# Block 0's input loaded and normalized by slots, and three edits of the early order

## The chip, the cores and the metric

The kernel runs on one core of one Trainium2 chip. Its time is the device time in microseconds (us) of one execution; the median of several runs is compared. The core has a matrix engine (TensorE, PE in the profile), a vector engine (VectorE, DVE), an activation engine (ScalarE, ACT), a general engine (GpSimd, POOL), a queue that issues most transfers (SyncE, SP), and 16 DMA engines that move the data. Each engine works through its own list of instructions in order, and waits for others by semaphores.

## The reference

A conditioned block of a transformer, for x of 2 x 2048 x 512 and a condition t of 2 x 512, all in f32:

```python
emb = silu(t) @ ada_w + ada_b                       # 512 -> 6 * 512
shift_msa, scale_msa, gate_msa, shift_mlp, scale_mlp, gate_mlp = split(emb, 6)
norm  = ln(x) * (1 + scale_msa) + shift_msa
h     = gelu(norm @ ssm_w1 + ssm_b1)                # 512 -> 512
x     = x + gate_msa * (h @ ssm_w2 + ssm_b2)        # 512 -> 512
norm2 = ln(x) * (1 + scale_mlp) + shift_mlp
hf    = gelu(norm2 @ ff_w1 + ff_b1)                 # 512 -> 1024
x     = x + gate_mlp * (hf @ ff_w2 + ff_b2)         # 1024 -> 512
```

`ln` subtracts the mean of the 512 features and divides by the root of the variance plus a small constant (1e-6; the kernel's EPS is 1e-5).

## The kernel before

The 4096 tokens are cut into eight blocks of 512. In a block each of the 128 partitions holds four tokens, one in each of four slots (`C = 4`), so that a slot is a 128 x 512 tile. A block passes four stages: `hA_i` (the first product of the SSM part, with gelu), `oA_i` (its second product, added to x), `hC_i` (the first product of the feed-forward part) and `oC_i` (the second). The products are done in f32 by schemes with fewer multiplications: a stage of type A has seven products P1 to P7 of half size, whose operands are sums of quarters; these sums are made by VectorE and GpSimd beside TensorE. `hC` has 26 products with sums called a (of the weights) and b (of the tokens).

Ahead of each type of product stands a LayerNorm (class `Norm`; `n1_i` ahead of hA_i, `n2_i` ahead of hC_i). Its steps are statistics (on VectorE by `bn_stats` and `bn_aggr`, or on ScalarE by a sum and a sum of squares with an accumulator), a root (`ve`, variance plus EPS, then a power of -0.5 on GpSimd), some small operations that sharpen the root by a Newton step and give `rstd` and `nmr`, the normalization of each slot, a transposition, and the modulation by scale and shift. For block 0's first norm the transposition is done by TensorE (`transpose`, L911) into four PSUM tiles `pts`; for the others by VectorE's turns (`turn`, L887) and transfers from `blocks` into `nT` (`move`, L895).

The modulation rows emb come from ada_w by small products on TensorE (`pada`). For the first two sixths they are made early: `rows_01` multiplies rows of 128 of ada_w (k = 0 to 3; `ada_01`), and `modulation_01` turns the result and adds the bias. The bias rows, cond and the other small vectors come in one tile `rows` by four small transfers on ScalarE's queue and are transposed on TensorE into `rowsT`, from which ScalarE copies them to `colsT`.

Until the first data are there TensorE multiplies the identity matrix by itself (`warm`, L1651).

The order of everything is written by hand. Loads stand on SP's queue in the order x_0 (two halves), ada's rows 0 and 1, 2, half of row 3, half of w1, the other half of row 3, the other half of w1, x_1, ada_2, four small gate biases, w2, b2, ada_3, ada_4, fw1. The transfers use eight semaphores in turn. From hA_0 on, `PLAN` names for each stage and each place behind a product (P1, P2, ...) which side operations are emitted there; `BY` names their engines. Names that matter here: `n1_1.stats`, `n1_1.root`, `n1_1.rest` (block 1's first norm), `gate_2.0` (modulation rows of the SSM gate and the addition of their bias on VectorE, L455) and `gate_2.1` (their spreading on TensorE, `pgate`, L462), `n1_1.sum` (operand sums of block 1), `n2_0.stats` (statistics of block 0's second norm), `n2_0.root`, `mods.0` and `mods.1` (the turned modulation rows 3 and 4 with their biases, L443 and L447), `rows.2` (modulation rows 5 on TensorE).

Lines that the trace names: L305 load of x, L348 and L355 of ada's first rows, L323 of w1, L336 to L339 the four small transfers, L418 `rows_01`, L431 and L435 `modulation_01`, L748 and L749 statistics on VectorE, L777 and L788 on ScalarE (sum, sum of squares), L812 and L813 the root, L836 to L840 block 0's small operations, L853 to L861 the others', L876 and L880 normalization, L932 and L934 modulation on ScalarE and VectorE, L500 operand sums, L709 the products of type A, L997 to L1021 what follows them, L1052 the addition to x.

Of the kernel before, what the change touches and what calls it, by code (L numbers as in the profile page):

```python
# [36 lines left out]
F32 = mybir.dt.float32  # L37
AF = mybir.ActivationFunctionType
ALU = mybir.AluOpType
EPS = 1e-06  # L40
# [103 lines left out]
        "P6": "n1_1.stats.5 n1_1.root.0 gate_2.0 n1_1.rest.0 n1_1.normal.0",  # L144
# [98 lines left out]
def kernel(  # L243
# [57 lines left out]
    def load_x(i, pieces=1):  # L301
        xs[i] = big_tile(f"x_{i}")
        for s in range(pieces):
            c = slice(s * C // pieces, (s + 1) * C // pieces)
            nc.sync.dma_start(out=xs[i][:, c, :], in_=x_blk[i][:, c, :])  # L305
# [38 lines left out]
    load_x(0, 2)  # L344
    ada_01 = [big_tile(f"ada_{h}").rearrange("p (k g) n -> p k (g n)", g=2) for h in range(2)]

    def load_ada_01(ks):
        nc.sync.dma_start(  # L348
            out=ada_01[ks[0] // 2][:, ks[0] % 2 : ks[-1] % 2 + 1],
            in_=ada_w[ks[0] * P : (ks[-1] + 1) * P, : 2 * D].rearrange("(k p) n -> p k n", p=P),  # L350
        )
# [8 lines left out]
    load_ada_01((0, 1))  # L360
    load_ada_01((2,))
# [373 lines left out]
    class Norm:  # L735
# [94 lines left out]
        def first_steps(self):  # L830

            n, v = self.name, nc.vector
            self.rstd, self.nmr = [small.tile([P, C], F32, tag=t, name=f"{t}{n}") for t in ("rstd", "nmr")]
            room = ps_t.tile([P, D], F32, tag="t", name=f"small{n}")
            a, b = room[:, :C], room[:, C : 2 * C]
            v.tensor_scalar(a, self.mv[:, :, 1], EPS, None, ALU.add)  # L836
            v.tensor_tensor(b, self.r, a, ALU.mult)
            v.scalar_tensor_tensor(b, b, -0.5, self.r, ALU.mult, ALU.mult)
            v.scalar_tensor_tensor(self.rstd, b, 1.5, self.r, ALU.add, ALU.mult)
            v.scalar_tensor_tensor(self.nmr, self.mv[:, :, 0], -1.0, self.rstd, ALU.mult, ALU.mult)  # L840
# [786 lines left out]
    def run(ops):  # L1627
        for op in ops:
            op()
# [19 lines left out]
    def warm(count, blocks=2):  # L1649
        for _ in range(count):  # L1650
            nc.tensor.matmul(  # L1651
                idle[:, :blocks],
                ident,
                ident.unsqueeze(1).to_broadcast([P, blocks, P]),
                start=True,
                stop=True,
            )

    warm(IDLE - 1, C)
    nc.tensor.transpose(pt[:, :ROWS], rows, ident[:ROWS, :ROWS])  # L1660
    warm(1, C)
    warm(1, 1)

    run(n1[0].stats())
    n1[0].root()
    nc.scalar.copy(colsT, pt[:, :ROWS])

# [3 lines left out]
        colsT[:, R_COND:R_ADA].rearrange("p (b k) -> p b k", b=B),  # L1671
        AF.Silu,
    )

    n1[0].first_steps()
# [3 lines left out]
    rows_01(pada_01, (0, 1))  # L1679
    for c in range(C):  # L1680
        n1[0].normal(c, nc.vector if c % 2 else None, on_pe=True)
    for g in (1, 4):
        rows_g = colsT[:, R_ADA + g * KD : R_ADA + (g + 1) * KD]
        nc.vector.tensor_scalar(rows_g, rows_g, 1.0, None, ALU.add)
# [113 lines left out]
    later("n2_0.stats", 9, lambda: sum(n2[0].split_stats(), []))  # L1798
# [411 lines left out]
```

## Time and profile before

| | us |
|---|---|
| median of 3 runs | 575.63 (575.44 to 576.18) |
| the profiled execution, in all | 576.39 |
| its span, first to last instruction | 574.3 |
| TensorE busy | 568.2 |
| first product of hA_0 | 14.10 |
| first product of hA_1 | 43.65 |

A row of the timeline gives the start in us, the duration, the engine, the line, the operation, out<-in, how many instructions are merged, and in brackets the idle time before and what released it. A row of the chain gives start, duration and what. The profile's engine "PE" is TensorE, "SPq" and "ACTq" are the instructions that issue transfers. A row of a table by windows gives the window, its length, the busy time of PE, PEld, DVE, ACT and POOL with the number of instructions, the granted clock of TensorE, the share of the DMA engines' time and GB/s. A row of waits gives who waited for whom: us in total, times, the longest.

### The profile page before, as it was taken

The numbers are of one execution on the slowest core, as the hardware profiler recorded it, in microseconds if no ns is written. First come the engines' busy times: TensorE is split into PE (matmuls) and PEld (weight loads), VectorE is DVE, ScalarE is ACT, GpSimd is POOL, SyncE is SP. The second block draws the span as 40 slices with busy tenths as digits, with TensorE's granted clock in tenths as the row PEclk, the third lists the DMA queues.
The fourth block names the chain that finished last, engine by engine and source line by source line (L and its number), as shares of the span: only waits on it lengthen the run. The fifth ranks groups of instructions, "written<-read, shape, count | busy, mean of one in ns | idle before, by whom it ended". The sixth has DMA issues, their size and how long they took to land.

```text
span 574.3 us, 10316 instructions
## 1 busy us (share of the span) xinstructions
PE 568.2 (99%) x3495; PEld 512.4 (89%) x3495; DVE 443.5 (77%) x992; ACT 306.2 (53%) x612; POOL 452.8 (79%) x477
## 2 busy tenths in 40 slices
PE   8999999999999999999999999999999999999997
PEld 4888888898899889998899988998889999899897
DVE  4898899657789376986869877996768588897676
ACT  2628559566834875448724688335655431732430
POOL 1699897996897869897899989998993888379261
PEclk9999999999999999999999999999999999999999
DMA  8968330414305503383032921242240240031002
GB/s 318 392 199 285 93 87 6 98 54 179 68 9 155 212 2 74 102 260 117 1 92 63 349 86 24 51 126 114 92 110 1 111 136 14 0 74 75 0 1 74
DMA packets 26992, 61.79 MB, mean 108 GB/s; under 512 B 5136, under 2 KB 6716, under 8 KB 25276
## 3 DMA queue, kind: packets, MB, share of 16 engines
q1 hardware_dynamic: 23040, 55.67, 30.0%
q10 hardware_dynamic: 3900, 5.47, 3.8%
q8 instruction: 28, 0.46, 0.3%
q14 instruction: 24, 0.20, 0.1%
HBM read 35.42 MB, written 9.97 MB: 79 GB/s over the span
## 4 chain that ended last, share of the span: by engine, by line
PE 97%; DMA 2%; DVE 0%; SPq 0%; ACT 0%; issue 0%; DVEq 0%
PE px_hC L1530 12%; PE pv_hC L1530 10%; PE py_hC L1530 10%; PE py_hA L709 9%; PE pl_oC_A_y L1364 5%; PE pv_hA L709 5%; PE py_oA L1091 5%; PE pl_oC_P_y L1204 4%; PE pl_oC_B_y L1364 4%; PE py_oA L709 4%; PE py_oC L1156 4%; PE pl_oC_A_v L1364 2%; PE px_hA L709 2%; PE pl_oC_P_v L1204 2%; PE pl_oA_y L1106 2%; PE pl_oC_B_v L1364 2%
## 5 line engine op out<-in xcount | busy, mean ns | idle before, releaser
L1435 POOL TENSOR_TENSOR forms<-forms 128x256 f32<-128x256 f32 x64 | 47.0, 735 | 3.8
L813 POOL TENSOR_TENSOR r<-ve,minus_half 128x4 f32<-128x4 f32 x16 | 16.6, 1037 | 41.4 <-DVE ve L812 33.8
L1530 PE MATMUL py_hC<-forms,fw 128*128 128x256 f32 x192 | 46.7, 380 | 0.0
L932 ACT ACTIVATE nT<-nT,mod,mod 128x512 f32<-128x512 f32 x31 | 22.9, 804 | 42.3 <-DMA nT<-blocks 34.3
L1530 PEld LDWEIGHTS py_hC<-forms,fw 128*128 128x128 f32 x192 | 36.3, 190 | 5.2 <-DVE hClo L1547 0.2
L1547 DVE TENSOR_TENSOR hClo<-hClo,py_hC 128x512 f32<-128x512 f32 x46 | 31.1, 682 | 10.6 <-ACT hClo L1544 7.4
L500 POOL TENSOR_TENSOR hSC<-hClo,hChi 128x512 f32<-128x512 f32 x14 | 18.0, 1286 | 27.0 <-ACT hChi L1525 24.8
L876 ACT ACTIVATE nT<-x,nmr,rstd 128x512 f32<-128x512 f32 x33 | 24.9, 804 | 18.8 <-DVE nmr L861 16.6
L1547 DVE TENSOR_TENSOR hChi<-hChi,pv_hC 128x512 f32<-128x512 f32 x38 | 25.2, 677 | 9.6 <-PE pv_hC L1530 5.3
L748 DVE BATCH_NORM_STATS2 st<-x 128x6 f32<-128x512 f32 x41 | 27.7, 677 | 5.6 <-DMA x<-in_x_dram 5.5
L1530 PE MATMUL px_hC<-forms,fw 128*128 128x256 f32 x128 | 31.5, 379 | 0.0
L1525 ACT ACTIVATE hClo<-hClo,colsT 128x256 f32<-128x256 f32 x64 | 28.8, 498 | 5.0 <-DVE hClo L1547 4.8
L1525 ACT ACTIVATE hChi<-hChi,colsT 128x256 f32<-128x256 f32 x64 | 28.7, 496 | 2.9 <-DVE hChi L1547 2.9
L1530 PEld LDWEIGHTS px_hC<-forms,fw 128*128 128x128 f32 x128 | 24.3, 190 | 3.3
L500 POOL TENSOR_TENSOR hClo<-hClo 128x512 f32<-128x512 f32 (+1 forms) x21 | 26.1, 1241 | 0.1
L1547 DVE TENSOR_TENSOR hChi<-hChi,px_hC 128x512 f32<-128x512 f32 x32 | 21.8, 682 | 4.4 <-ACT hClo L1544 2.1
L932 ACT ACTIVATE x<-x,mod 128x512 f32<-128x512 f32 x24 | 17.6, 802 | 13.4 <-DMA x<-blocks 13.4
L887 DVE STREAM_TRANSPOSE blocks<-nT 128x512 f32<-128x512 f32 x36 | 24.0, 691 | 0.7 <-ACT nT L876 0.7
L1530 PE MATMUL px_hC<-forms,fw_s 128*128 128x256 f32 x96 | 23.6, 382 | 0.0
L1544 ACT ACTIVATE hClo<-px_hC 128x512 f32<-128x512 f32 x22 | 13.1, 596 | 19.5 <-PE px_hC L1530 16.0
L1547 DVE TENSOR_TENSOR hClo<-hClo,px_hC 128x512 f32<-128x512 f32 x26 | 17.6, 677 | 7.6 <-PE px_hC L1530 7.0
L1530 PE MATMUL pv_hC<-nT,fw 128*128 128x256 f32 x96 | 23.3, 379 | 0.0
(588 smaller groups left out, 1904.5 us busy)
## 6 DMA issues: line engine op xcount, KB each, us to landing
x<-in_x_dram SPq DMA_DIRECT2D x13, 1024.0 KB
out_dram<-x SPq DMA_DIRECT2D x14, 512.0 KB
x<-blocks SPq DMA_DIRECT2D x93, 64.0 KB
nT<-blocks SPq DMA_DIRECT2D x88, 64.0 KB
ada<-in_L_cond_ada_w_dram SPq DMA_DIRECT2D x5, 1024.0 KB
fw<-in_L_cond_ff_w_dram SPq DMA_DIRECT2D x2, 2048.0 KB
nT<-blocks ACTq DMA_DIRECT2D x56, 64.0 KB
w<-in_L_cond_ssm_w_dram SPq DMA_DIRECT2D x2, 1024.0 KB
```

Of the source, the lines that this page charges most:

```text
L500: eng.tensor_tensor(out[:, r], a[:, r], b[:, r], f)
L709: nc.tensor.matmul(ps[b][j * apart][:, j, :], lhs(p, j, k), rhs(p, j, k), start=(fresh and j * (not apart) == 0 and k == 0), stop=(p in (" ...
L748: nc.vector.bn_stats(st, xs[self.i][:, c, :])
L876: nc.scalar.activation(t, x_c, AF.Identity, bias=self.nmr[:, c : c + 1], scale=self.rstd[:, c : c + 1])
L932: nc.scalar.activation(dst, src, AF.Identity, bias=shift, scale=scale)
L1091: nc.tensor.matmul(ps[BANK[p]][:, j, :], hops(p, j, k), wops[p][:, k, :], start=False, stop=(k == KD // 2 - 1), skip_group_check=True,)
L1204: nc.tensor.matmul(t[:, n, :], hops.leaves[p][f][:, k, :], leaf_wops[p][f][:, k, :], start=room not in started, stop=(f in ("P2", "P3", "P ...
L1364: nc.tensor.matmul(rooms[g, b][:, at[p], :], hops.leaves[p][f][:, k, :], leaf_wops[p][f][:, k, :], start=(g, b) not in started, stop=(f in ...
L1435: eng.tensor_tensor(reg[d], reg[a], reg[b], ALU.add if f == "+" else ALU.subtract)
L1525: nc.scalar.activation(h, h, AF.Gelu_apprx_tanh, bias=fb1T[:, m : m + 1])
L1530: nc.tensor.matmul(ps[b][:, j, :], fa[ra][:, j * P : (j + 1) * P], fb[rb].rearrange("p a (c q) -> p c a q", q=Q), start=(fresh and j == 0) ...
L1547: nc.vector.tensor_tensor(dest(d), dest(d), ps[b], op)
```

## The change

- Block 0's x is loaded in four transfers, one for each slot, instead of two; ada's rows 0 and 1 by two transfers instead of one.
- The condition's part of the small vectors is transposed on TensorE by itself, ahead of the rest, and goes to silu from PSUM; the rest is copied as before. The additions of 1 to the scale biases move from VectorE to GpSimd. TensorE's warm-up is two products of four blocks shorter ahead of the transposition (one follows the condition's), and one product of one block is left out behind it.
- Block 0's first norm is done by halves of two slots: root and small operations once for each half, and normalization of a half behind its own. On TensorE the transposes of slots 1 and 0 now stand ahead of ada's row 2, those of 3 and 2 behind the first half of row 3.
- In hA_0 behind P6, `gate_2.0` stands ahead of `n1_1.root.0`.
- `n2_0.stats`: the statistics of slot 2 move from ScalarE (sum, bias, squares) to VectorE; slots 0 and 1 stay on ScalarE, slot 3 on VectorE.
- `n2_0.root` stands ahead of `n1_1.sum.3` behind hA_1's P1.
- `mods.1` moves from the end of oA_0 to hA_1 behind P6.

```diff
-        "P6": "n1_1.stats.5 n1_1.root.0 gate_2.0 n1_1.rest.0 n1_1.normal.0",
+        "P6": "n1_1.stats.5 gate_2.0 n1_1.root.0 n1_1.rest.0 n1_1.normal.0",
...
-        "P4": "n2_0.stats.2 n2_0.stats.8 a.9 n2_0.stats.4 mods.1 gates.0",
+        "P4": "n2_0.stats.2 n2_0.stats.6 n2_0.stats.5 a.9 n2_0.stats.4 gates.0",
...
-        "start": "n1_1.sum.1 n2_0.stats.5 n2_0.stats.6 a.13 a.14",
-        "P1": "n2_0.stats.3 n1_1.sum.3 n2_0.stats.7 n2_0.root.0 a.10",
+        "start": "n1_1.sum.1 n2_0.stats.3 a.13 a.14",
+        "P1": "n2_0.root.0 n1_1.sum.3 a.10",
...
-        "P6": "n2_0.rest.0 n2_0.normal.0 rows.2 n2_0.normal.3",
+        "P6": "n2_0.rest.0 n2_0.normal.0 rows.2 n2_0.normal.3 mods.1",
...
-    load_x(0, 2)
+    load_x(0, C)
...
-    load_ada_01((0, 1))
-    load_ada_01((2,))
+    for k in range(KD - 1):
+        load_ada_01((k,))
...
+        def first_root(self, h):
+
+            n, v, s = self.name, nc.vector, slice(h * C // 2, (h + 1) * C // 2)
+            if h == 0:
+                self.ve, self.r, self.rstd, self.nmr = [
+                    small.tile([P, C], F32, tag=t, name=f"{t}{n}") for t in ("ve", "r", "rstd", "nmr")
+                ]
+                self.first_room = ps_t.tile([P, D], F32, tag="t", name=f"small{n}")
+            v.tensor_scalar(self.ve[:, s], self.mv[:, s, 1], EPS, None, ALU.add)
+            nc.gpsimd.tensor_tensor(self.r[:, s], self.ve[:, s], minus_half[:, s], ALU.pow)
+            v.tensor_scalar(self.first_room[:, s], self.mv[:, s, 1], EPS, None, ALU.add)
+
+        def first_steps(self, h):
...
+            v.tensor_tensor(b, r, a, ALU.mult)
+            v.scalar_tensor_tensor(b, b, -0.5, r, ALU.mult, ALU.mult)
+            v.scalar_tensor_tensor(rstd, b, 1.5, r, ALU.add, ALU.mult)
+            v.scalar_tensor_tensor(nmr, self.mv[:, s, 0], -1.0, rstd, ALU.mult, ALU.mult)
...
-    warm(IDLE - 1, C)
+    warm(IDLE - 3, C)
+    turned_cond = pt[:, ROWS : ROWS + B * KD]
+    nc.tensor.transpose(turned_cond, rows[R_COND:R_ADA], ident[: B * KD, : B * KD])
+    warm(1, C)
     nc.tensor.transpose(pt[:, :ROWS], rows, ident[:ROWS, :ROWS])
     warm(1, C)
-    warm(1, 1)
...
+    stats = n1[0].stats()
+    run(stats[:2])
+    n1[0].first_root(0)
+    run(stats[2:])
+    for g in (1, 4):
+        rows_g = colsT[:, R_ADA + g * KD : R_ADA + (g + 1) * KD]
+        nc.gpsimd.tensor_scalar(rows_g, rows_g, 1.0, None, ALU.add)
+    n1[0].first_root(1)
     w1_ops, w1_sums, w1_s = weight_of_first("w1", w1_sb)
     run(w1_sums)
+    for h in range(2):
+        n1[0].first_steps(h)
+        for c in (3 * h, 1 + h):
+            n1[0].normal(c, nc.vector if c % 2 else None, on_pe=True)
...
+    rows_01(pada_01, (0, 1))
+    n1[0].transpose(1, pts, True)
+    n1[0].transpose(0, pts, False)
     rows_01(pada_01, (2,))
-    n1[0].transpose(1, pts, True)
     rows_01(pada_01, (3,), (0,))
-    for c in (0, 3, 2):
-        n1[0].transpose(c, pts, c == 3)
+    n1[0].transpose(3, pts, True)
+    n1[0].transpose(2, pts, False)
...
-    later("n2_0.stats", 9, lambda: sum(n2[0].split_stats(), []))
+    later("n2_0.stats", 7, lambda: sum(n2[0].mixed_stats(2), []))
```

`mixed_stats` was there before; it gives, for the number of slots named, the sums, the bias and the squares on ScalarE, and `bn_stats` with `bn_aggr` on VectorE for the other slots.

More of the change, by code (lines that the diff above doesn't have):

```diff
@@ L828, in rest @@
             v.tensor_scalar(self.nmr, self.nmr, -1.0, None, ALU.mult)
[L830 to L840, printed above, removed]
+        def first_root(self, h):
[9 more added lines that the diff above has]
+        def first_steps(self, h):
+            v, s = nc.vector, slice(h * C // 2, (h + 1) * C // 2)
+            a, b = self.first_room[:, :C][:, s], self.first_room[:, C : 2 * C][:, s]
+            r, rstd, nmr = self.r[:, s], self.rstd[:, s], self.nmr[:, s]
+            v.tensor_tensor(b, r, a, ALU.mult)
+            v.scalar_tensor_tensor(b, b, -0.5, r, ALU.mult, ALU.mult)
+            v.scalar_tensor_tensor(rstd, b, 1.5, r, ALU.add, ALU.mult)
+            v.scalar_tensor_tensor(nmr, self.mv[:, s, 0], -1.0, rstd, ALU.mult, ALU.mult)
         def steps(self, scratch=None):
@@ L1657, in warm @@
             )
[L1659 removed]
+    warm(IDLE - 3, C)
+    turned_cond = pt[:, ROWS : ROWS + B * KD]
+    nc.tensor.transpose(turned_cond, rows[R_COND:R_ADA], ident[: B * KD, : B * KD])
+    warm(1, C)
     nc.tensor.transpose(pt[:, :ROWS], rows, ident[:ROWS, :ROWS])
     warm(1, C)
[L1662 to L1666 removed]
     nc.scalar.activation(
         silu[:, :, :B].rearrange("p k b -> p b k"),
[L1671 removed]
+        turned_cond.rearrange("p (b k) -> p b k", b=B),
         AF.Silu,
     )
[L1675 removed]
+    nc.scalar.copy(colsT[:, R_ADA:], pt[:, R_ADA:ROWS])
+    stats = n1[0].stats()
[6 more added lines that the diff above has]
+    n1[0].first_root(1)
     w1_ops, w1_sums, w1_s = weight_of_first("w1", w1_sb)
     run(w1_sums)
+    for h in range(2):
+        n1[0].first_steps(h)
+        for c in (3 * h, 1 + h):
+            n1[0].normal(c, nc.vector if c % 2 else None, on_pe=True)
     pada_01 = ps_t.tile([P, D], F32, tag="t", name="pada_01")
[L1679 to L1684, printed above, removed]
     pts = {
```

## The prediction, made before the result was known

> **What bounds the kernel now.** I read the page first, then the chain that ended last in order of time, then the timeline of the first 50 us engine by engine, the waits of SP's queue, and the DMA view in short windows.
>
> ```profile
> span 574.3 us, 10316 instructions
> PE 568.2 (99%) x3495; PEld 512.4 (89%) x3495; DVE 443.5 (77%) x992; ACT 306.2 (53%) x612; POOL 452.8 (79%) x477
> PE 97%; DMA 2%; DVE 0%; SPq 0%; ACT 0%; issue 0%; DVEq 0%
> ```
>
> TensorE (PE) is the bound. Only two kinds of time can move: the start, before PE has work, and the few places where PE later waits for something. All edits lie in the first 60 us.
>
> ```profile
> 2.10 9.07 DMA ada<-in_L_cond_ada_w_dram
> 11.22 0.64 PE pada L418 x16
> 12.80 1.47 PE pt L911 x12
> 16.12 0.57 ACT nT L932
> 16.74 1.99 PE px_hA L709 x8
> ```
>
> The chain shows the start: until 11.17 it is a transfer of ada, then the modulation rows and transposes on PE, then VectorE (DVE) and ScalarE (ACT) making nT, and the second product of hA_0 at 16.74. From there PE runs on, but at the next stage it is not PE that sets the time:
>
> ```profile
> 41.74 1.89 PE L709 MATMUL py_oA<-w_s,forms 128*128 128x256 f32 x8
> 43.65 1.99 PE L709 MATMUL py_hA<-nT,w 128*128 128x256 f32 x8
> 42.78 2.23 ACT L932 ACTIVATE nT<-nT,mod 128x512 f32<-128x512 f32 x3 [10.59 <-DMA fw_t<-in_L_cond_ada_b_dram]
> 35.28 5.78 ACTq L895 DMA_DIRECT2D nT<-blocks  x8
> 26.00:35.20 9.20, 9.20 (x45) 8.09 (x44) 9.17 (x18) 5.73 (x10) 5.90 (x5) 1.00 0.77 299
> 26.23 0.15 DVE L861 SCALAR_TENSOR_TENSOR nmr<-mv,small 128x4 f32<-128x4 f32 x1
> 24.48 1.02 POOL L813 TENSOR_TENSOR r<-ve,minus_half 128x4 f32<-128x4 f32 x1 [1.20 <-DVE ve L812]
> 24.23 0.17 DVE L812 TENSOR_SCALAR ve<-mv 128x4 f32<-128x4 f32 x1 [1.32 <-ACT unread L788]
> 17.95 0.63 ACT L777 ACTIVATE unread<-x 128x512 f32<-128x512 f32 x1 [0.81 <-DMA x<-in_x_dram]
> ```
>
> Read from the top, backwards. The products of oA_0 that begin at 41.74 come at 0.216 us each (1.73 us for eight, as the chain has them), so PE was free at 43.47; hA_1 began at 43.65, and its group took 1.99 against 1.89, the 0.10 of a restart. It waited for ACT's first modulation of block 1, 42.78 plus about 0.8. ACT waited for the moves of nT (the row names another transfer; the eight of its own queue were issued until 41.06 and are the last needed). They began at 35.28, after VectorE's turns. VectorE was busy 9.17 of the 9.20 us before that, from the end of block 1's LayerNorm at 26.38, which hangs on GpSimd's (POOL's) root, that on ACT's statistics, and those on block 1's x having landed at about 17.9. **So hA_1 begins some 25.8 us after x_1 lands, whatever PE does before, and PE's slack there is negative (0.18).** A start that is 0.3 us earlier is given back at 43.65; a later x_1 passes to the end nearly in full.
>
> **The change part by part.** First, x_0 in four transfers of 256 KB and ada's rows 0 and 1 apart: three transfers more on SP, none of them more bytes.
>
> ```profile
> 0.72 0.86 SPq L305 DMA_DIRECT2D x<-in_x_dram  x2
> 1.63 1.04 SPq L348 DMA_DIRECT2D ada<-in_L_cond_ada_w_dram  x2
> SPq L323 <- DMA x<-in_x_dram: 1.5, 1, 1.5
> SPq L355 <- DMA fw_t<-in_L_cond_ada_b_dram: 1.6, 1, 1.6
> GB/s 0 53 266 189 376 385 391 418 401 350 372 381 398 442 408 406 389 385 385 389 385 385 387 389 387 375 385 410 401 420 389 418 270 53 8 16 100 129 203 203
> DMA packets 271, 1.02 MB, mean 407 GB/s; under 512 B 21, under 2 KB 23, under 8 KB 271
> DMA packets 621, 1.16 MB, mean 386 GB/s; under 512 B 57, under 2 KB 57, under 8 KB 621
> ```
>
> The fifth row has slices of 1 us from 0 to 40; the last two are 6.5 to 9 us (pieces of 4 KB) and 17 to 20 us (2 KB). From 4 to 32 us the DMA engines run at their rate, so x_1 lands when the bytes ahead of it are through. Those bytes are unchanged; what changes is that x_0's pieces are 2 KB, not 4 KB. 1.05 MB cost 2.72 us at 386 and 2.58 at 407: **+0.14** if the engines are the limit then. From 2 to 4 us they moved 266 and 189, so something else limits part of it, and the cost may be nothing. A gain isn't excluded: 0.9 us of full-rate work is missing in those two slices, and smaller first pieces may fill some; I bound it at half, -0.45. I take +0.1, nearest to the row of 2 KB pieces. Issue costs about 0.43 each, so x and the first ada are issued by 2.9, before 4 us.
>
> The Trainium skill ("DMA: Bandwidth & Descriptors", Measured) speaks against this: transfers should be batched to 1 MiB or more, since each has about 2.0 us fixed. By it, three more transfers one after another would cost 6 us; with this case's transfers overlapping on one queue (418 GB/s in the slice after 7 us), the trace doesn't agree, and by the row the sum is +0.1.
>
> The wait rows fit one rule: a transfer is issued when the one eight places ahead of it has landed (ACT's four small ones of cond and the biases are counted in). So w1's first half waited for x's first half, the last piece of ada for ada_b's rows. With three more ahead, ada's second row comes to wait for a slot of x and its third probably for ada_b's rows. That is rival B; the cover is that x and ada's first two rows, 2.1 MB, take until 8.0 us by the slices.
>
> Second, **the LayerNorm of x_0 by two slots**, its rows and transposes reordered.
>
> ```profile
> 10.35 0.17 DVE L837 TENSOR_TENSOR small<-r,small 128x4 f32<-128x4 f32 x1 [1.14 <-POOL r L813]
> 11.14 1.52 ACT L876 ACTIVATE blocks<-x,nmr,rstd 128x512 f32<-128x512 f32 x2 [2.02 <-DVE nmr L840]
> 12.38 0.43 PE L418 MATMUL pada<-ada,w_t 128*32 128x128 f32 x8
> 13.49 1.27 ACT L932 ACTIVATE nT<-pt,mod 128x256 f32<-128x256 f32 x2 [0.82 <-PE pt L911]
> 14.10 0.70 PE L709 MATMUL py_hA<-nT,w 128*128 128x256 f32 x2
> 14.30 0.54 DVE L934 TENSOR_SCALAR nT<-pt,mod 128x256 f32<-128x256 f32 x1 [0.26 <-PE pt L911]
> ```
>
> It adds a second set of six small VectorE operations (about 0.2 each, 1.2 us) and a second root (1.0 us on GpSimd), and moves two small additions to GpSimd (about 0.2 each by GpSimd's small operations of 0.19 to 0.20 elsewhere). All fall before 11 us, in VectorE's wait of 1.14 and beside ada's transfer; without that cover the small operations would cost their 1.2. The first two slots can be normalized before 11 us, the last two by 11.9 at worst (GpSimd's root after its additions), not 12.66 (11.14 + 1.52). Then transposes of slots 1 and 0 can run in PE's idle time before 11.2, and only eight remain after the row at 12.38, not twelve: at 1.47 for twelve, 0.49 less. hA_0's first product doesn't gain: 14.10 hangs on 12.38 (ada's last row landing), the turn, the sum and ACT's 13.49 + 0.57. But VectorE's operation at 14.30 waited 0.26 for the transposes. Without it the sum nS, the second turn and nT behind it move up by 0.26 and the product at 16.74 to 16.48; that is where the eight products from 14.10 end (1.73 for them, 0.43 as at 12.38 for the modulation rows between, 0.2 for two restarts: 16.46), so a third restart of 0.10 may go too: **0.26 to 0.36 us earlier**. What stalls next is hA_1's wait: it takes all of this, and 0 is left at the end.
>
> Third, the swap of gate_2.0 and n1_1.root. VectorE's addition for the gate no longer stands behind ve at 24.23, which waits for ACT. ve itself waits as before, so GpSimd's root at 24.48 and everything behind it stay. PE's gate product has 0.2 us more air, needed only if PE is earlier. 0.
>
> Fourth, **slot 2's second statistics to VectorE**, the root ahead of n1_1.sum.3, and the modulation mods.1 later.
>
> ```profile
> 45.35 0.70 DVE L748 BATCH_NORM_STATS2 st<-x 128x6 f32<-128x512 f32 x1
> 46.18 0.30 DVE L443 STREAM_TRANSPOSE pada<-pada 128x128 f32<-128x128 f32 x1
> 47.22 0.61 ACT L777 ACTIVATE unread<-x 128x512 f32<-128x512 f32 x1
> 49.61 0.17 DVE L812 TENSOR_SCALAR ve<-mv 128x4 f32<-128x4 f32 x1 [1.15 <-ACT unread L788]
> 49.69 0.69 DVE L1007 TENSOR_TENSOR hA<-px_hA,hA 128x512 f32<-128x512 f32 x1
> 50.75 1.08 PE L397 MATMUL pada<-ada,w_t 128*32 128x128 f32 x32
> ```
>
> ACT loses a sum (0.61), a bias and a square pass, all of them between 47.22 and ve at 49.61, about 1.5 us: it is done near 48.1. VectorE gains one slot's statistics, 0.83 (45.35 to 46.18, the same for another slot), and loses mods.1, some 0.4 from 46.18. So its next addition is 0.4 later and ve can run near 48.15, 1.45 earlier, with GpSimd's root behind it. sum.3 now stands behind ve, and behind sum.3 the addition at 49.69 that reads px. With 0.7 to 1.2 for the sum px is read by 49.7 to 50.3 (50.38 before). PE's modulation rows at 50.75 may now need px's room, since mods.1 holds the other one longer: 0.45 of slack. The three modulations that mods.1 serves come in oA_1, several us on. PE's products keep their places: 0. Bounds: -0.2 (GpSimd's root comes 1.4 earlier, and with it its sums, where PE may wait for them behind 60 us; one such wait taken as large as hA_1's 0.18), +0.5 (px read 0.9 later than I work out, less the slack).
>
> **The sum**: 0 (start) + 0.1 (x_1) + 0 + 0. The profiled execution has span 574.3 and took 576.39 in all, so 2.1 lie around it; that execution was 0.76 over the median of the runs, 575.63. Against that median: 575.7.
>
> **The rivals.**
> A, the wait at hA_1 yields: the ramp of the first 4 us fills better, x_1 lands up to 0.45 earlier and PE's own 0.35 lets it use this. For: the slices 266 and 189. Against: from 4 us on nothing is free. 575.63, less the wait of 0.18, its restart of 0.10 and the start's 0.36: 575.0.
> B, the slower side: **ada's third row waits for ada_b's rows and the DMA engines run dry.**
>
> ```profile
> 6.88 0.37 SPq L355 DMA_DIRECT2D ada<-in_L_cond_ada_w_dram  x1
> 8.23 0.34 SPq L305 DMA_DIRECT2D x<-in_x_dram  x1
> ```
>
> ada_b's rows had landed by 6.88, the issue that waited for them; bytes come about 1 us after an issue (none in the first slice, for an issue at 0.72), so 7.9, against 8.0 when the queue is empty. Decides from a landing at 7.0; each us behind that puts x_1 and hA_1 one us later. If these rows land as late as the last bias row that x_1's issue waited for (8.23), it is 1.2 us: 576.9. Against: with smaller pieces ahead of them they should land sooner.
> C, the addition that reads px ends after 50.75 because its room is now held, or VectorE is late: 0.5 us over what I worked out: 576.2.
> D, the shorter warm-up (six passes for eight ahead of the rows, and one small product fewer behind them) lets PE's clock fall.
>
> ```profile
> 1.34 5.93 PE L1651 MATMUL idle<-w_t 128*128 128x512 f32 x8 [1.34 <-POOL w_t masks.py:199]
> 8.35 0.23 PE L1660 MATMUL rowsT<-w_t,fw_t 44*128 44x44 f32 x1 [1.08 <-DMA fw_t<-in_L_cond_ff_b_dram]
> ```
>
> PE idled 1.08 us before 8.35 without harm; two of the eight passes fewer make it 2 to 3. At half the clock the PE work from 11.22 to 16.74, some 5 us, costs up to 2.5 more, less 0.5 of lost gain and slack: 577.6. The Trainium skill ("TensorE: Matmul & The Clock Gate", Part 1) has the clock halved after an idle window of about 3.4 us; by it D doesn't come about, and the trace (1.00 granted throughout) agrees.
> E, the change shifts nothing at all, its start gain lost and no packet cost: 575.6, inside the forecast.
>
> **Chances.** Forecast with E 0.72, A 0.12, B 0.07, C 0.07, D 0.02. Range 574.9 to 576.6: from a little past A to past C, leaving D, most of B and the tails out. About 0.2% (1.15 us) is what a measurement of this kernel can tell from no change: faster than 574.5 needs more than A, 0.07; slower than 576.8 is B's far end and D, 0.07; within, 0.86.
>
> **What would show it.** hA_0's second product near 16.5 and its first still near 14.1; block 1's statistics on ACT beginning at 17.9 to 18.1; hA_1 still after ACT's modulation, at 43.6 to 43.9, with a larger idle gap of PE before it; ve of n2_0 near 48.2. I would be wrong if block 1's x landed over 0.5 us earlier or later, if hA_1 no longer waited for ACT, or if PE stalled anew between 50 and 90 us.

## The result and the profile after

The changed kernel is slower: 578.09 us in the median against 575.68, ratio 1.0032 [1.0022, 1.0042]; repeated, 577.17 against 575.85, 1.0023 [1.0013, 1.0033]. I had forecast 575.7. Its profiled execution got a mean TensorE clock of 0.557 and took 998 us (without it the first median is 577.96, and the ratios leave it out), so the trace shown here is that of the repeat (577.00 us, clock 0.999).

The kernel before, too, was profiled again (575.71 us), since the execution on which the prediction rests was 0.7 us above the median. These two traces are compared from here on. (Lines behind L830 stand ten further down in the changed kernel: L932 is L942 there, L1014 is L1024.) The kernel before: the page's head, then the DMA engines' GB/s in slices of 1 us from 0, then rows of the timelines of ScalarE, VectorE and TensorE.

```profile
span 573.6 us, 10316 instructions
```
```profile
GB/s 0 32 242 254 396 375 386 410 414 371 354 394 396 444 420 399 371 391 385 391 379 383 391 393 375 385 377 404 416 410 401 414 262 33 16 53 199 197 195 207
```
```profile
17.21 0.63 ACT L777 ACTIVATE unread<-x 128x512 f32<-128x512 f32 x1 [0.91 <-DMA x<-in_x_dram]
23.50 0.17 DVE L812 TENSOR_SCALAR ve<-mv 128x4 f32<-128x4 f32 x1 [1.42 <-ACT unread L788]
25.55 0.68 DVE L1014 TENSOR_TENSOR forms<-py_hA,forms 128x512 f32<-128x512 f32 x1
...
13.27 0.70 PE L709 MATMUL py_hA<-nT,w 128*128 128x256 f32 x2
15.90 1.99 PE L709 MATMUL px_hA<-nT,w 128*128 128x256 f32 x8
26.83 1.89 PE L709 MATMUL py_hA<-nS,w 128*128 128x256 f32 x8
28.56 1.89 PE L709 MATMUL py_oA<-w,forms 128*128 128x256 f32 x8
30.29 1.89 PE L709 MATMUL px_oA<-w,forms 128*128 128x256 f32 x8
32.01 1.89 PE L709 MATMUL pv_oA<-w_s,hSA 128*128 128x256 f32 x8
42.73 1.89 PE L709 MATMUL py_hA<-nT,w 128*128 128x256 f32 x8
```

The same views of the changed kernel, with the row ahead of L1024 besides:

```profile
span 575.1 us, 10322 instructions
```
```profile
GB/s 0 25 248 249 243 284 324 399 406 415 385 386 378 384 434 428 375 385 385 388 389 385 393 371 385 387 387 387 416 399 406 422 393 188 20 16 33 117 211 197
```
```profile
18.30 0.63 ACT L777 ACTIVATE unread<-x 128x512 f32<-128x512 f32 x1 [1.52 <-DMA x<-in_x_dram]
24.57 0.17 DVE L812 TENSOR_SCALAR ve<-mv 128x4 f32<-128x4 f32 x1 [1.38 <-ACT unread L788]
26.56 0.15 DVE L871 SCALAR_TENSOR_TENSOR nmr<-mv,small 128x4 f32<-128x4 f32 x1
26.62 0.68 DVE L1024 TENSOR_TENSOR forms<-py_hA,forms 128x512 f32<-128x512 f32 x1
...
14.07 0.70 PE L709 MATMUL py_hA<-nT,w 128*128 128x256 f32 x2 [0.35 <-DMA fw_t<-in_L_cond_ada_b_dram]
16.45 1.92 PE L709 MATMUL px_hA<-nT,w 128*128 128x256 f32 x8
27.45 1.96 PE L709 MATMUL py_hA<-nS,w 128*128 128x256 f32 x8
29.36 1.99 PE L709 MATMUL py_oA<-w,forms 128*128 128x256 f32 x8
31.20 1.97 PE L709 MATMUL px_oA<-w,forms 128*128 128x256 f32 x8
33.01 1.24 PE L709 MATMUL pv_oA<-w_s,hSA 128*128 128x256 f32 x5
43.82 1.99 PE L709 MATMUL py_hA<-nT,w 128*128 128x256 f32 x8
```

The slices tell most of it. From 4 to 7 us the engines moved 243, 284 and 324 GB/s where they had moved 396, 375 and 386: 306 KB less, 0.8 us at 385. So ada's rows and x_1 come later, block 1's statistics begin at 18.30 instead of 17.21 (+1.09; 0.3 of it these slices do not account for), and the root's `ve` runs at 24.57 instead of 23.50. That reaches TensorE soon. On VectorE, L1024, which reads hA_0's results out of PSUM, stands in order behind block 1's `nmr` (26.56). It ends at 27.30, and TensorE's group at 27.45 follows it; in the kernel before it ended at 26.23, 0.6 ahead of that group (26.83). From there TensorE's groups start 1.91, 1.84 and 1.81 us apart where they had been 1.73 apart. hA_0's second product is 0.55 later, hA_1 1.09 later (43.82 for 42.73).

Of these 1.09 us some 0.6 are gone again by 325 us, in small waits that the kernel before has from 59 us on and the changed one, later, does not. The other step is at 361 us, +1.03 on TensorE. Rows of the timeline there, first of the changed kernel, then of the kernel with x_0 in halves (e1 below), both with VectorE and GpSimd starting within 0.03 us of each other:

```profile
360.40 1.78 DVE L500 TENSOR_TENSOR fw<-fw 128x512 f32<-128x512 f32 x1
360.37 1.26 POOL L500 TENSOR_TENSOR hSC<-hSC,hClo 128x512 f32<-128x512 f32 x1
363.30 0.49 PE L1116 MATMUL pl_oA_y<-w,hA 128*128 128x128 f32 x2 [0.77 <-DVE x L1131]
```

```profile
360.00 0.68 DVE L500 TENSOR_TENSOR fw<-fw 128x512 f32<-128x512 f32 x1
360.00 1.81 POOL L500 TENSOR_TENSOR hSC<-hSC,hClo 128x512 f32<-128x512 f32 x1
361.97 0.39 PE L1116 MATMUL pl_oA_y<-w,hA 128*128 128x128 f32 x2
```

In e1, where both start at 360.00, VectorE's operation took 0.68 and GpSimd's 1.81; where GpSimd's was first by 0.03, VectorE's took 1.78, and TensorE waited 0.77 for what stood behind it. No other trace at full clock lost time at this place, so in this execution it is bad luck. Whether the change made the tie so close is not shown: VectorE starts 0.34 to 0.36 ahead in both traces of the kernel before and in e4, but the two start within 0.06 in 11 of the 15 traces of the changed kernel and its variants.

A third part shows only in the times. 6 of 20 executions of the changed kernel (the two of 998 and 3051 us left out) had a mean clock of 0.997, and took 578.6 in the mean; the other 14 have a median of 576.9. In 109 executions of the kernel before none was below 0.999. 0.3% of 576 is 1.7 us, as much as one window of 3.4 us at half clock costs (e7 below shows one).

### The profile page after: what moved, and what is told of

Same layout as the page of the kernel before. It is cut to its first block, busy times and chain, and to the rows that moved or that the text cites. A ratio compares the mean times of both kernels' runs of the same rounds, so it can differ in the third digit from the quotient of the medians.

```text
span 996.2 us, 10322 instructions
## 1 busy us (share of the span) xinstructions
PE 990.3 (99%) x3492; PEld 700.2 (70%) x3492; DVE 454.6 (46%) x998; ACT 310.9 (31%) x607; POOL 450.8 (45%) x480
## 4 chain that ended last, share of the span: by engine, by line
PE 99%; DMA 1%; DVE 0%; issue 0%
PE px_hC L1540 12%; PE py_hA L709 10%; PE py_hC L1540 10%; PE pv_hC L1540 10%; PE pl_oC_A_y L1374 5%; PE pv_hA L709 5%; PE py_oA L1101 5%; PE py_oA L709 4%; PE pl_oC_B_y L1374 4%; PE py_oC L1166 4%; PE pl_oC_P_y L1214 4%; PE pl_oC_A_v L1374 2%; PE px_hA L709 2%; PE pl_oA_y L1116 2%; PE pl_oC_P_v L1214 2%; PE pv_oA L709 2%
## 5 line engine op out<-in xcount | busy, mean ns | idle before, releaser
L1540 PE MATMUL py_hC<-forms,fw 128*128 128x256 f32 x192 | 80.1, 581 | 0.0
L1540 PEld LDWEIGHTS py_hC<-forms,fw 128*128 128x128 f32 x192 | 43.0, 224 | 30.5 <-issue 17.9
L1540 PE MATMUL px_hC<-forms,fw 128*128 128x256 f32 x128 | 54.2, 577 | 0.0
L1540 PEld LDWEIGHTS px_hC<-forms,fw 128*128 128x128 f32 x128 | 29.3, 229 | 19.5 <-issue 10.3
L1540 PE MATMUL px_hC<-forms,fw_s 128*128 128x256 f32 x96 | 40.0, 585 | 0.0
L1540 PE MATMUL pv_hC<-nT,fw 128*128 128x256 f32 x96 | 39.9, 583 | 0.0
L709 PE MATMUL py_hA<-x,w 128*128 128x256 f32 x96 | 39.3, 582 | 0.0
L1445 POOL TENSOR_TENSOR forms<-nT,forms 128x256 f32<-128x256 f32 x31 | 22.6, 741 | 28.2 <-ACT nT L942 19.2
L942 ACT ACTIVATE nT<-nT,mod,mod 128x512 f32<-128x512 f32 x31 | 22.9, 803 | 37.0 <-DMA nT<-blocks 28.5
L1101 PE MATMUL py_oA<-w,hA 128*128 128x256 f32 x80 | 32.7, 582 | 0.0
L1540 PEld LDWEIGHTS px_hC<-forms,fw_s 128*128 128x128 f32 x96 | 22.0, 229 | 15.1 <-issue 6.5
```

The lines of the kernel that those rows point to most:

```text
L709: nc.tensor.matmul(ps[b][j * apart][:, j, :], lhs(p, j, k), rhs(p, j, k), start=(fresh and j * (not apart) == 0 and k == 0), stop=(p in (" ...
L942: nc.scalar.activation(dst, src, AF.Identity, bias=shift, scale=scale)
L1101: nc.tensor.matmul(ps[BANK[p]][:, j, :], hops(p, j, k), wops[p][:, k, :], start=False, stop=(k == KD // 2 - 1), skip_group_check=True,)
L1445: eng.tensor_tensor(reg[d], reg[a], reg[b], ALU.add if f == "+" else ALU.subtract)
L1540: nc.tensor.matmul(ps[b][:, j, :], fa[ra][:, j * P : (j + 1) * P], fb[rb].rearrange("p a (c q) -> p c a q", q=Q), start=(fresh and j == 0) ...
```

## The experiments

**e1, e2, e3: which part.** The changed kernel with x_0 in halves again, with the long warm-up again, with both.

```diff
-    load_x(0, C)
+    load_x(0, 2)          # e1, e3
```
```diff
-    warm(1, C)            # behind the condition's transposition
+    warm(2, C)            # e2, e3
 ...
+    warm(1, 1)            # e2, e3: behind the rows
```

> The changed kernel with x_0 in two transfers again (4 KB pieces), all else kept. Theory 1 (pieces of 2 KB make the queue move some 250 GB/s instead of 380 between 2 and 8 us, so that x_1 lands 1.1 us later, and hA_1 hangs on x_1): x_1 lands at 17.8 to 18.0 as before, hA_1 begins near 43.6, and executions whose TensorE clock is full all the way take 575.4 to 575.8. Theory 2 (it is the number of transfers, ada's second and third row waiting for earlier landings): x_1 still lands about 1 us late, near 18.9, 576.8. Theory 3 (the edits behind hA_1 cost): x_1 early, but 576.8 all the same. On the clock: if the window at half clock comes from the shorter warm-up alone, it is still seen in part of the executions; if it comes from the late data, it is gone.

> The changed kernel with its warm-up as long as before (a product of four blocks more ahead of the rows, one of one block more behind them), x_0 still in four transfers. If the shorter warm-up is what lets the clock fall to a half for one window of 3.4 us, the executions near 578.2 vanish and all take 576.7 to 576.9 at a granted clock of 1.00; if the later data alone do it, executions near 578.2 stay.

> Both undone: x_0 in halves and the warm-up as before, with the norm by two slots, the reordered transposes and the three edits of the plan kept. Theory 1 with the clock's: 575.3 to 575.8, no different from before (the start's gain of some 0.3 us ends at hA_1's wait). Theory 2: 576.8. Theory 3: over 576.2 though hA_1 begins near 43.6.

Measured: e1 576.06, ratio 1.0000 [0.9991, 1.0009]; e2 577.23, 1.0023 [1.0014, 1.0032]; e3 575.91, 1.0000 [0.9991, 1.0009]. The whole loss goes with x_0's slots. What e3 keeps (LayerNorm by two slots, ada's two transfers, the swap, the statistics, the root, mods.1) is worth nothing, and the length of the warm-up does not change the median (e1 and e3 agree). In e2, though, none of 11 executions had a clock of 0.997. Rows of e1's timelines:

```profile
17.20 0.63 ACT L777 ACTIVATE unread<-x 128x512 f32<-128x512 f32 x1 [1.09 <-DMA x<-in_x_dram]
...
13.40 0.70 PE L709 MATMUL py_hA<-nT,w 128*128 128x256 f32 x2 [0.35 <-ACT nT L942]
...
15.78 1.49 PE L709 MATMUL px_hA<-nT,w 128*128 128x256 f32 x6
...
43.22 1.99 PE L709 MATMUL py_hA<-nT,w 128*128 128x256 f32 x8 [0.40 <-ACT nT L942]
```

x_1 is back at 17.20, as before, and hA_1 waits 0.40 for ScalarE's modulation, as the prediction said it would when TensorE is early.

**e4: the slots alone**, put into the kernel before.

```diff
-    load_x(0, 2)
+    load_x(0, C)
```

> The kernel before with x_0 in four transfers and nothing else. Theory 1: x_1 lands 0.9 to 1.1 us later than before and the whole is that much later, 576.5 to 576.8, with the old norm and the old ada transfers. Theory 2 (the split of ada and its waits): nearly as before, 575.6 to 575.9. The clock should hold, since the warm-up is the long one.

577.50, ratio 1.0032 [1.0022, 1.0042]; statistics of block 1 at 18.85, hA_1 at 44.37. One word of the change makes all of its loss. Here, though, the start alone is enough for it: ada's rows come late, TensorE waits 1.5 us for one of them, hA_0 begins at 15.00 instead of 13.27, and at hA_1 there is no wait.

**e7: the landing by itself.** x_0 in halves, x_1 behind ada's third block.

```diff
-    load_x(0, C)
+    load_x(0, 2)
...
-    load_x(1)
     load_ada(2)
+    load_x(1)
```

> The changed kernel with x_0 in halves (576.1 by itself) and block 1's x loaded behind ada's third block instead of ahead of it: 1 MB, about 2.6 us later, with everything of block 0 as it was. If hA_1 hangs on this landing: statistics on ScalarE at 19.6 to 20.0, hA_1 at 45.3 to 46.0, less the 0.4 that PE already waits there: 578.1 to 578.7. If block 1's landing has air and what x_0 by slots costs lies in block 0's own start: within 0.4 of 576.1.

580.76. The direction is right, the size is not: x_1 came at 21.03, a microsecond later than I had worked out, and the loss took another place. Rows of the timelines of ScalarE and TensorE, and the windows around them (column after the engines: granted clock):

```profile
21.03 0.63 ACT L777 ACTIVATE unread<-x 128x512 f32<-128x512 f32 x1 [4.03 <-DMA x<-in_x_dram]
...
30.20 3.65 PE L709 MATMUL py_hA<-nS,w 128*128 128x256 f32 x8 [2.61 <-DVE forms L1024]
```

```profile
26.00:30.00 4.00, 1.59 (x8) 1.06 (x6) 1.51 (x9) 1.74 (x5) 1.02 (x1) 1.00 1.03 397
30.30:33.60 3.30, 3.30 (x8) 2.67 (x9) 3.30 (x7) 2.81 (x6) 1.81 (x2) 0.50 0.80 319
33.70:37.00 3.30, 3.30 (x17) 2.91 (x16) 2.67 (x4) 2.25 (x4) 2.71 (x3) 1.00 0.03 11
```

TensorE waited 2.61 for L1024, the same place as the small delays in the changed kernel, and then worked 3.4 us at half clock: 8 products in 3.3 us, and 17 in the next 3.3. This trace is 5.7 longer than that of e1 (4.7 in the medians); the wait and the half clock are some 2.6 and 1.7 of it, and 1.0 comes behind hA_1, which was not followed up. The clock was 0.997 in all of its four executions.

**Why the slots land late: size of the pieces, or number of transfers.** Seven other cuttings of x_0 were compared with the change by what the DMA engines moved from 2 to 8 us. All move the same 1 MB first.

```diff
-    load_x(0, C)
+    xs[0] = big_tile("x_0")
+    # e5: s, q in 2 x 2           xs[0][q * 64 : q * 64 + 64, 2 * s : 2 * s + 2]
+    # e6:                         load_x(0)
+    # e9: q in 4                  xs[0][q * 32 : q * 32 + 32]
+    # e10: s in 2                 xs[0][:, s::2]
+    # e13: s, q in 2 x 2          xs[0][q::2, 2 * s : 2 * s + 2]
+    # e14: q in 4                 xs[0][q::4]
```

> The changed kernel with x_0 still in four transfers of 256 KB, but each of 64 partitions by two slots, so that the pieces are 4 KB as before (the first statistics then wait for two transfers). If the size of the pieces costs the microsecond: the slices from 3 to 6 us are near 400 GB/s as with halves, block 1's statistics begin at 17.1 to 17.6, the time is 575.8 to 576.3. If it is the number of transfers on the queue: they begin at 18.6 to 19.0 and the time is 577.0 to 577.6.

> The changed kernel with x_0 in one transfer of 1 MB, pieces of 8 KB: the other way from halves. If larger pieces fill the first microseconds better still: block 1's statistics at 16.5 to 17.0; but VectorE's statistics of block 0 then begin only at about 5.8, with room before ada's third row, so the time is 575.5 to 576.0. If 4 KB is already enough: statistics at 17.1 to 17.4 and 575.8 to 576.2. If the start is now bound by block 0's LayerNorm: hA_0's first product after 14.0 and 576.3 or more.

> The changed kernel with x_0 in four transfers of 256 KB, each of 32 partitions, pieces of 8 KB (the first statistics wait for all four). If the size of the pieces sets the rate: 2.2 to 2.35 MB moved by 8 us, as with one transfer (2.31). If it is the number of transfers or how many partitions each covers: 1.3 to 1.75 MB by 8 us, as with the four of 4 KB on 64 partitions (1.33) and the four of 2 KB (1.63 to 1.75), and 577 or more.

> The changed kernel with x_0 in two transfers of 512 KB over all 128 partitions, the first with slots 0 and 2 and the second with 1 and 3, so that the pieces are 2 KB but the transfers two. If the size of the pieces sets the rate: 1.65 to 1.75 MB by 8 us, statistics of block 1 at 18.3 to 18.9, 576.8 to 577.3. If the number of transfers does: 2.05 to 2.1 MB as with halves, statistics at 17.1 to 17.6, 576.0 to 576.4.

> Again the changed kernel with x_0 in four transfers of 256 KB and pieces of 4 KB, but each of every second partition instead of the lower or the upper 64, so that all of the 128 partitions' range is written at once. If the two halves of the partitions were what slowed e5 (225 GB/s from 2 to 8 us): 300 or more here. If the number of transfers is the cause: 230 to 295, with the time at 576.8 or more. If the size of the pieces is: 335 to 350 as with two transfers of 4 KB, and 576.0 to 576.6.

> The same for pieces of 8 KB: four transfers, each of every fourth partition. Partitions together as the cause of e9's 231 GB/s: 300 or more from 2 to 8 us. Number of transfers: 230 to 295. Size of the pieces: 370 or more, as with the one transfer of 8 KB pieces (377).

The DMA view of 2 to 8 us, one row each: e6, e1, e10, the changed kernel, e5, e13, e9, e14.

```profile
DMA packets 535, 2.26 MB, mean 377 GB/s; under 512 B 72, under 2 KB 108, under 8 KB 415
```
```profile
DMA packets 618, 2.07 MB, mean 346 GB/s; under 512 B 80, under 2 KB 116, under 8 KB 618
```
```profile
DMA packets 807, 1.84 MB, mean 306 GB/s; under 512 B 71, under 2 KB 107, under 8 KB 807
```
```profile
DMA packets 810, 1.75 MB, mean 291 GB/s; under 512 B 101, under 2 KB 137, under 8 KB 810
```
```profile
DMA packets 449, 1.35 MB, mean 225 GB/s; under 512 B 88, under 2 KB 124, under 8 KB 449
```
```profile
DMA packets 469, 1.42 MB, mean 236 GB/s; under 512 B 92, under 2 KB 128, under 8 KB 469
```
```profile
DMA packets 344, 1.39 MB, mean 231 GB/s; under 512 B 88, under 2 KB 124, under 8 KB 230
```
```profile
DMA packets 435, 1.76 MB, mean 293 GB/s; under 512 B 102, under 2 KB 138, under 8 KB 307
```

| x_0 as | pieces | GB/s, 2 to 8 us | time | ratio |
|---|---|---|---|---|
| one transfer (e6) | 8 KB | 377 | 576.40 | 1.0008 [1.0000, 1.0017] |
| two (e1) | 4 KB | 346 | 576.06 | 1.0000 [0.9991, 1.0009] |
| two (e10) | 2 KB | 306 | 578.36 | 1.0049 [1.0032, 1.0065] |
| four (the change) | 2 KB | 291 | 577.17 | 1.0023 [1.0013, 1.0033] |
| four, 64 partitions each (e5) | 4 KB | 225 | 578.45 | 1.0036 [1.0023, 1.0049] |
| four, every second partition (e13) | 4 KB | 236 | 577.83 | 1.0034 [1.0021, 1.0046] |
| four, 32 partitions each (e9) | 8 KB | 231 | 580.42 | 1.0080 [1.0068, 1.0092] |
| four, every fourth partition (e14) | 8 KB | 293 | 579.43 | one execution |

The times of e5, e9, e10 and e13 hold windows at half clock in most executions (see rival D below), so the rate is the measure here, not the time.

My first theory, that the size of the pieces alone counts, falls: with four transfers no size of piece came above 293. But that the number alone counts is not shown either. Each transfer covers all 128 partitions only in e6, e1, e10 and the change. Among these, two transfers lose 40 GB/s when their pieces go from 4 to 2 KB (346, 306), and 2 KB pieces lose another 15 when the transfers go from two to four (306, 291). All the traces with halves have 338 to 349, all four with these slots 271 to 291, and of e10 there is one. e10 met neither expectation: its block 1 begins at 18.01, between the two. So both seem to have a part, and the size of the pieces not the smaller one.

e5, e9, e13 and e14 keep large pieces and are slow all the same, but each of their transfers covers only a part of the partitions, which may slow it for a reason of its own. With every second or fourth partition (e13, e14) 11 and 62 GB/s more were moved than with neighbouring ones. From 4 to 7 us the DMA engines were busy all the time in e5 and e9 (share 1.01), but only 0.83 and 0.87 of it in e13 and e14. What stands is that each finer cut of the first 1 MB moved less than the whole. The slices of e10 show that 2 KB pieces can be fast: from 4.5 to 5.5 us, when its x_0 was still coming,

```profile
DMA packets 202, 0.37 MB, mean 366 GB/s; under 512 B 19, under 2 KB 25, under 8 KB 202
```

e6 moves most, yet is not faster: VectorE must wait for the whole of x_0, its statistics begin at 5.56 instead of 4.81, and TensorE idles 1.22 us for the first normalized slot. That answers the expected gain of a better start (rival A): the ramp can be filled, by larger pieces and not by smaller ones, but not for nothing.

**e11, e12, e15: four transfers at another time.**

```diff
-    load_x(0, C)
+    load_x(0, 2)            # e11, e15
-    load_x(1)
+    load_x(1, C)            # e11, in its place; e15: ahead of ada's first row
...
+    load_ada_01((0,)); load_ada_01((1,))      # e12: ahead of load_x(0, C)
```

> The changed kernel with x_0 in halves and block 1's x in four transfers of 256 KB by slots, in the middle of the stream. If four transfers of one block slow the DMA engines anywhere: the slices from 14 to 17 us fall from 385 to about 250 GB/s, the last slot lands 1.3 us or more later than the 17.2 of a single transfer, and the time is 577 or more. If they slow them only in the first microseconds: the slices stay near 385 and the time is that of two halves of x_1, 575.2 to 575.7.

> The changed kernel with ada's first two rows issued ahead of x_0's four slots, to see the rate alone (the start itself comes later: some 578 to 581). If the slow rate belongs to the first microseconds of a kernel: ada's two rows come at some 300 GB/s as x_0's halves did, and x_0's four slots behind them at 380 or more. If it belongs to the four transfers: the first slices are near 400 and those in which x_0's slots come, from about 4 to 8 us, fall to about 250.

> The changed kernel with x_0 in halves and x_1's four slots right behind it, ahead of ada (the start comes later for it, 577 to 580). If four 2 KB transfers are slow in the first 8 us whatever block they carry: 250 to 300 GB/s in the slices from 5 to 7 us. If it is a matter of x_0 alone, the first transfers of the kernel: 380 or more there, as in the middle of the stream (388).

e11: from 14.5 to 17 us, with x_1's four 2 KB slots passing,

```profile
DMA packets 522, 0.97 MB, mean 388 GB/s; under 512 B 48, under 2 KB 48, under 8 KB 522
```

and 575.45, ratio 0.9996 [0.9987, 1.0006]. e12, 3 to 5 us (ada's rows) and 5.5 to 7.5 us (x_0's slots behind them):

```profile
DMA packets 248, 0.80 MB, mean 399 GB/s; under 512 B 31, under 2 KB 56, under 8 KB 248
...
DMA packets 292, 0.51 MB, mean 254 GB/s; under 512 B 39, under 2 KB 46, under 8 KB 292
```

e15, 5 to 7 us (x_1's slots behind x_0's halves):

```profile
DMA packets 327, 0.59 MB, mean 296 GB/s; under 512 B 54, under 2 KB 66, under 8 KB 327
```

So it isn't x_0 and it isn't the very first transfers: four transfers of 256 KB in 2 KB pieces are slow (254 to 296) among the first few on the queue, and as fast as any (388) where the queue has long been full. Besides, e12 (580.06) pays for its late x_0, for which TensorE waits 3.3 us, and e15 (580.54) for its late ada rows (1.9).

One rival is that the engines ran out of packets, since each further transfer also takes SP longer to issue (1.85 us for four, 0.87 for two). The shares of the DMA engines' time speak against it, here first for e12, 5.5 to 7.5 us, then for e11, 14.5 to 17 us:

```profile
q1 hardware_dynamic: 277, 0.50, 95.5%
```
```profile
q1 hardware_dynamic: 522, 0.97, 105.2%
```

In e12 the engines had packets nearly all the time, but a packet of about the same size took longer: 110 ns against 81 (share times window times 16 engines, by the number of packets). Why it takes longer there is open; the traces don't show what a DMA engine waits for.

**e8: block 1's x in halves** (x_0 in halves too), so that ScalarE can begin early if a split costs nothing there.

```diff
-    load_x(0, C)
+    load_x(0, 2)
...
-    load_x(1)
+    load_x(1, 2)
```

> The changed kernel with x_0 in halves (576.1) and x_1 in halves as well, in its place, so that ScalarE can begin block 1's statistics with the first slots 1.3 us ahead of the last byte. If the chain behind x_1 sets hA_1: statistics at 15.9 to 16.2, the last of the three sums some 0.9 us earlier, the 0.4 that PE waited at hA_1 gone: 575.5 to 575.8, faster than both kernels. If another transfer on the queue costs DMA rate here as it did for x_0: the last byte later by 0.5 or more and 576.1 to 576.6.

575.32 against 575.66, ratio 0.9991 [0.9982, 1.0000]. Statistics from 16.09, hA_1 at 42.33, without a wait:

```profile
16.09 0.63 ACT L777 ACTIVATE unread<-x 128x512 f32<-128x512 f32 x1
...
42.33 1.89 PE L709 MATMUL py_hA<-nT,w 128*128 128x256 f32 x8
```

With e11 (575.45) it is the fastest kernel here, 1.9 us below the changed one, and 0.3 below the kernel before, at the edge of what was measured.

**The kernel before and the changed kernel once more.**

> The kernel before once more, unaltered, since its first profiled execution was 0.7 us above its median. If x_1's landing also scatters there and sets the time: statistics on ScalarE at 17.1 to 17.6 instead of 17.95, hA_1 at 43.0 to 43.4 instead of 43.65, span 573.5 to 574.0. If the first trace was typical at its start and lost elsewhere: statistics again at 17.9 to 18.0 and hA_1 at 43.6.

> The changed kernel once more, unaltered, for a trace at full clock. If block 1's landing sets the time, its statistics begin on ScalarE at 18.9 to 19.0 (17.2 in the kernel with x_0 in halves), hA_1 begins 25.5 to 26.0 us later, at 44.4 to 45.0, and 530.7 us follow it: a span of 575.1 to 575.7. If the start's order were at fault by itself, hA_1 would come more than 26.0 us after the landing, or more than 530.9 us would follow it.

575.84, and 577.17 as above. x_1's landing scatters (17.95 and 17.21 in the two traces of the kernel before), and hA_1 follows it by 25.52 us in the new traces of both kernels. In the kernel before the landing was where it was expected to be if it sets the time, hA_1 0.3 earlier; in the changed one both came 0.6 earlier than expected, and 531.3 us followed hA_1 instead of 530.7, for the near tie at 361.

## Why the prediction was wrong

**The step that failed is "I take +0.1" for x_1's landing.** I priced x_0's pieces by two rows of a full queue, 386 and 407 GB/s, and bounded the cost at +0.14. In the stretch where x_0 really moves the changed kernel had 243 to 324 against 375 to 396, and x_1 landed 1.09 later (1.64 in e4, 1.74 in e2, which have the same slots). The medians rose by 1.3 to 1.6 in e4, e2 and the repeat. The row nearest in kind (2 KB pieces) was far away in the state of the queue, and that state decides: 388 in the middle of the stream (e11), 291 at the start, both with 256 KB transfers of 2 KB pieces. With it a second term failed, the 0 for the start: slower slots delay ada's rows too, and hA_0 began at 14.07 instead of 13.27. The slices of 266 and 189, which I took for a ramp that smaller pieces might fill, were the warning.

I also set a rule aside there that I should have kept as a rival. The Trainium skill ("SBUF — State Buffer", The DMA setup-cost knee) gives 224 GB/s for transfers of 256 KiB and 341 for 1 MiB, on account of a fixed cost of each; that is the same thing as the rule of batching to 1 MiB that I quoted and rejected with the slice at 7 us. At the start the traces agree with it in kind (four 225 to 293, two 306 to 346, one 377 GB/s), though the size of the pieces has a part in these numbers; in the middle of the stream they don't (388). Rejecting it by a row from 7 us was the mistake; the start is where the traces agree with it.

**The mechanism behind the step held in part.** Begin of hA_0, of block 1's statistics, and of hA_1:

| | hA_0 | statistics | hA_1 | statistics to hA_1 | hA_1 to the end |
|---|---|---|---|---|---|
| before, first trace | 14.10 | 17.95 | 43.65 | 25.70 | 530.7 |
| before, second trace | 13.27 | 17.21 | 42.73 | 25.52 | 530.9 |
| e1 | 13.40 | 17.20 | 43.22 | 26.02 | 530.8 |
| e8 | 13.29 | 16.09 | 42.33 | 26.24 | 531.0 |
| the change | 14.07 | 18.30 | 43.82 | 25.52 | 531.3 |
| e4 | 15.00 | 18.85 | 44.37 | 25.52 | 530.8 |
| e2 | 14.75 | 18.95 | 44.80 | 25.85 | 530.9 |
| e7 | 14.28 | 21.03 | 47.87 | 26.84 | 531.8 |

A later x_1 goes with a later hA_1 and a later end, nearly in full, as forecast; in the kernel before, the first trace was 0.74 later at x_1 and 0.7 longer. But the start was later in it too, by 0.83, and so it is in e4 and e2. That x_1's landing does it by itself is shown by e7 alone, where TensorE waited for what stands behind it. Which chain ended last shows in one distance: where hA_1 hangs on ScalarE's modulation it begins 0.87 after the modulation begins (the first trace of the kernel before, the change, e1, e2, e7); it is 0.90 to 1.25 in the second trace, e4 and e8, and there TensorE's own work ended last. In the change ScalarE came last by 0.1 only, since L1024 had held TensorE up as well. "Whatever PE does before" was too strong. The 0.18 by which TensorE waited at hA_1 belongs to that one execution; in the second there is no wait. Both chains, the start's and x_1's, hang on the same stream of transfers and are mostly within 0.5 of each other at hA_1, so what delays the stream delays both. And the delay reaches TensorE earlier than I wrote: at 27 us, because L1024 stands on VectorE behind block 1's root.

**The start by two slots** did what was worked out: from hA_0's first product to its second it is 2.38 us (14.07 to 16.45) for 2.63 (13.27 to 15.90), 0.25 less, for 0.26 predicted; e1 has 2.38 too. As predicted it is worth 0 at the end (e1, e3). That 14.07, 16.45 and 43.82 are also near the times that I gave (14.1, 16.48, 43.6 to 43.9) is chance: mine came from a late execution.

**The plan edits** cost nothing (e3: 1.0000). `ve` of n2_0 was to run near 48.2 and ran at

```profile
48.22 0.75 DVE L812 TENSOR_SCALAR ve<-mv 128x4 f32<-128x4 f32 x1 [0.25 <-ACT unread L788]
```

and TensorE has no new wait between 44 and 90 us. Rival C did not come. Of B the wait came, but early: ada's third row waited 0.8 for ada_b's rows and was issued at 5.1, long before the 7.0 from which B would have counted, and x_1's issue waited for none.

**Rival D came in part**, and by another road. Its half clock is in 6 of 20 executions, one window and 1.7 us each. But e4 with the whole warm-up has it too (2 of 9), and with the short one e1 hardly (1 of 11) and e11 not at all (0 of 10). With the short one and data that come late it is frequent: e7 4 of 4, e9 5 of 5, e10 5 of 6, e13 4 of 6, and e5, whose TensorE waited 2.20 us for ada, 4 of 5. In e5's trace, by windows:

```profile
8.60:11.80 3.20, 1.29 (x32) 0.78 (x32) 2.64 (x11) 0.12 (x1) 1.60 (x4) 1.00 1.02 399
11.90:15.20 3.30, 2.92 (x28) 2.51 (x32) 1.44 (x6) 1.42 (x2) 0.00 (x0) 0.50 1.07 376
```

TensorE was 1.29 of 3.20 us busy in the first stretch, and got half clock in the next. So the window goes with late data more than with the short warm-up. In e2, with late data and a longer warm-up, none of 11 had it; whether the warm-up protects is left open, since e4 speaks against it.

## What to carry to other kernels

Price a transfer by rows from its own stretch: with few transfers ahead of it on the queue, cutting 1 MB into four slots made a later transfer land 1.1 to 1.7 us later here; in the middle of a full queue the same cut was free and let the consumer begin 1.3 us early (e11, 15.88 for 17.20). Take two traces of the kernel before a term of some tenths is built on one wait: the wait of 0.18 from which this prediction started was gone in the next execution. And follow a late operation through the queue of its engine: what stands behind it in order is late too, whether it needs the data or not.

## What was not expected of the hardware

- One execution of the changed kernel was granted a mean clock of 0.557, full for the first 5 us and 0.5 to 0.56 from there on (998 us); one of e8 0.656 (849 us); one of the changed kernel took 3051 us at full clock.
- VectorE and GpSimd shut each other out in some operations on SBUF: 0.68 against 1.78 us for the same addition, decided by 0.03 us. The Trainium skill ("SBUF — State Buffer", SBUF: two separate sides) calls it an exclusive lock of a shared port, held for the whole instruction; the two rows at 360 us agree nearly (VectorE's ends 0.55 after GpSimd's, where it takes 0.68 alone).
- TensorE's clock was halved for one window of 3.4 us after waits of 2.2 (e5) to 2.6 us (e7), shorter than the idle window of 3.4 us by which the prediction set rival D aside.
